# A four-layer graph network on one core: layer 2's edges in fixed chunks of 128, with the lock lookup moved into layer 1's experts

## The chip, the core and the metric

The kernel runs on one core of one Trainium2 chip. A core has a matrix unit (TensorE, PE; its loads of stationary operands are listed as PEld), VectorE (DVE), ScalarE (ACT), GpSimd (POOL) and SyncE (SP), each with an instruction list of its own that it works off in order, and DMA queues which are filled by SP, ACT and GpSimd. The metric is the device time of one execution, in microseconds (us). All data is fp32 unless said otherwise.

## The reference, cut to what matters

3125 nodes with 256 features, 100000 edges (source, destination, weight), sorted by destination. A layer is a graph convolution plus a mixer, added to x, and then a mixture of experts, added to x. Four such layers follow each other, of different kinds. The change touches two places: layer 1's experts, which every node passes through (8 experts, three 256 x 256 products each),

```
h = relu(bn(x @ W1[e] + b1[e])); h = relu(bn(h @ W2[e] + b2[e])); x += w[e] * (h @ Wo[e] + bo[e])
```

and the graph convolution of layer 2, which prunes small messages except into locked nodes:

```
norm_node_in = norm(x, axis=0);  norm_all_in = norm(norm_node_in) / 256
W_eff  = where(abs(W) < 0.1 * norm_all_in / norm_node_in, 0, W)
h      = x @ W_eff.T
lock   = locked[dst] | (src == dst)
msg    = edge_weight[:, None] * h[src]
n      = norm(msg, axis=1)
msg    = where((n < 0.1 * sum(n) / E) & ~lock, 0, msg)
out    = segment_sum(msg, dst) + b
```

Here `locked` marks the nodes of a list of 1000. The destinations are drawn as 3125 times the square of a uniform number, so low-numbered nodes have far more edges than high-numbered ones. Destinations and sources are known only on the device; what the program knows when it is built is their distribution.

## The kernel before

**Blocks and pieces.** Nodes lie in 25 blocks of 125 (`x[125, 25, 256]`, one node per partition), and are handled in seven pieces of four blocks (the last piece has one). `xt` is the same with the features on the partitions.

**PSUM.** `bank()` gives out PSUM banks from one pool of four in turn. A bank is free again when the instruction that reads its product out has run. The graph convolution of layer 2 has two accumulators of its own (`acc`).

**Layer 1's experts** (`l1_ffn`). For each expert and piece: products into h1, ScalarE evacuates them with the relu (L1411), products into h2, ScalarE again (L1416), then one product per block, which VectorE adds into x (L1422, scalar_tensor_tensor). The weights of an expert are loaded ahead from SP and ACT. After the last expert each piece is normed and transposed for layer 2 (`last`), one piece behind.

**Layer 2's preparation** (`l2_prepare`) is a generator which `l1_ffn` advances twice. First, before the experts, it issues the loads: GpSimd fetches the edge records (packed destination and source, and the weight) with 25 indirect DMAs, one per block (L1445), each with room for the most edges that the block can have. `ROOM` holds these sizes, in columns of 128 edges: 841 columns in all, where 100000 edges need 782; the rest is filled with edges of other blocks, which no target of the block matches. Second, after expert 1, it builds the lock table: `locked` from eight small products (L1464), then `lock`, one row of 125 flags per block broadcast over the partitions (L1471, L1473). The decoding of the records (L1477 to L1488) is written there too, but in VectorE's list it stands before the first update of the first expert.

**Layer 2's graph convolution** (`l2_gnn`). Fourteen Squares over `xt` on ScalarE (L1503) give the norms, W is pruned, h is computed per block and written to DRAM with its row norm as a 257th column (`hx`). Then the gather loop: for each block, in groups of up to eight columns (`CPG`), GpSimd gathers 128 rows of `hx` per column (L1551) into `hg`, of which there are four buffers. VectorE forms `keep` for the group (L1555, L1556) from the row norms, and for each column the 128 x 125 matrix `to`: first weight where the edge's target is this column of the block (L1560, tensor_scalar), then times the larger of lock and keep (L1562, scalar_tensor_tensor). PE multiplies `to` with the gathered rows into the block's accumulator (L1564; each fp32 product is two instructions in the profile). At the end of a block VectorE adds the accumulator into x (L1566).

**Order of the work.** `together` runs the gather loop and layer 2's mixer as two generators and always advances the one that reports the smaller share done. Each engine's list then follows from the order in which the program emits instructions, moved a little by the tool that lays them out; on the chip every engine takes its list in order and waits on semaphores. `prep`, at the very start, finds the first edge of each block and counts violations of the assumed room in `viol`; if there is one, the program at the end runs `general`, a second version of the network without such assumptions.

Of the kernel before, what the change touches and what calls it, by code (L numbers as in the profile page):

```python
# [12 lines left out]
F32 = mybir.dt.float32  # L13
I32 = mybir.dt.int32
# [3 lines left out]
AF = mybir.ActivationFunctionType  # L18
OP = mybir.AluOpType
AX = mybir.AxisListType  # L20
PSUM = bass.MemoryType.PSUM
DRAM = bass.MemoryType.DRAM

N = 3125
D = 256
P = 125
NB = 25
HB = D // 128
E = 100000
# [13 lines left out]
def _room(d0, d1):  # L43


    m = E * (math.sqrt(d1 / N) - math.sqrt(d0 / N))
    return max(1, math.ceil((m + 4 * math.sqrt(m) + 1) / 128))
# [18 lines left out]
NT1 = -(-NE1 // 128)  # L66
ROOM = [_room(b * P, b * P + P) for b in range(NB)]
NC2 = sum(ROOM)

# [19 lines left out]
class Net:  # L89
    NE, TS = 16, 384  # L90

    def __init__(self, tc, a, ctx):
# [13 lines left out]
        nc.vector.memset(self.ones, 1.0)  # L106
        self.iota_f = c.tile([128, 128], F32, name="iota_f")
        nc.gpsimd.iota(self.iota_f, pattern=[[1, 128]], base=0, channel_multiplier=0,
                       allow_small_or_imprecise_dtypes=True)
# [170 lines left out]
    def prep(self):  # L280

        nc, a = self.nc, self.a
        self.rec_d = self.dram.tile([1, 2 * EP], F32, name="rec_d")
        self.viol = self.c.tile([128, 8], F32, name="viol")
        self.tab = self.c.tile([128, 4, NT1 + 1], F32, name="tab")
        self.idx1 = self.c.tile([128, NT1], I32, name="idx1")
        self.idx2 = self.c.tile([128, NB], I32, name="idx2")
        nc.vector.memset(self.viol, 0.0)
        nc.scalar.dma_start(self.tab, nc.inline_tensor(_tables(), name="windows").ap())
        room = np.stack([np.broadcast_to(np.array(ROOM) * 128.0, (128, NB)),  # L290
                         np.arange(128)[:, None] * 2.0 * np.array(ROOM)], 1).astype(np.float32)
        with ExitStack() as s:
            sb = s.enter_context(self.pool("p_sb"))
            wk = s.enter_context(self.pool("p_wk", 3))
            rm = sb.tile([128, 2, NB], F32, name="rm")
            nc.scalar.dma_start(rm, nc.inline_tensor(room, name="room").ap())
            dst = sb.tile([128, EC], I32, name="dst")
# [70 lines left out]
            gap2 = sb.tile([128, NB], F32, name="gap2")  # L368
            nc.vector.tensor_sub(gap2, sr[:, 1:], sr[:, :NB])
            nc.vector.tensor_tensor(gap2, gap2, rm[:, 0, :], op=OP.is_gt)  # L370
            nc.vector.tensor_reduce(self.viol[:, 2:3], gap2, axis=AX.X, op=OP.add)
            i2 = sb.tile([128, NB], F32, name="i2")
            nc.vector.scalar_tensor_tensor(i2, sr[:, :NB], 2.0, rm[:, 1, :], op0=OP.mult, op1=OP.add)
            nc.vector.tensor_scalar(self.idx2, i2, float(2 * EP - 1024), None, op0=OP.min)

# [982 lines left out]
    def l1_ffn(self, before, after):  # L1358
# [4 lines left out]
        with ExitStack() as s:  # L1363
# [25 lines left out]
            def last(i, w):  # L1389
                self.norm_turn_piece(i, w)  # L1390

                x = self.x[:, i // P:(i + w) // P]
                nc.vector.tensor_add(x, x, self.e2["bias"][:P, None, :].to_broadcast([P, w // P, D]))

            self.expect(2, follow, 1)
# [36 lines left out]
    def l2_prepare(self, sb, wk):  # L1432
# [3 lines left out]
        e = self.e2 = {}  # L1436
        e["w"] = self.load_w(sb, "L2_gnn_W")
        li = wk.tile([P, LOCKS // P], I32, name="li", bufs=1)
        nc.scalar.dma_start(li, a["L2_gnn_node_lock"])
        bias = self.load_b(sb, "L2_gnn_b")  # L1440
        bo = self.load_b(wk, "L2_mix_b_out", eng=nc.sync)
        rec = wk.tile([128, NC2, 2], F32, name="rec_b", bufs=1)
        c0 = np.cumsum([0] + ROOM).tolist()
        for b in range(NB):
            nc.gpsimd.indirect_dma_start(  # L1445
                out=rec[:, c0[b]:c0[b + 1]].rearrange("p c t -> p (c t)"), out_offset=None, in_=self.rec_d,
                in_offset=bass.IndirectOffsetOnAxis(ap=self.idx2[:, b:b + 1], axis=1))
        yield
# [10 lines left out]
        for j in range(LOCKS // P):  # L1459
# [4 lines left out]
            nc.tensor.matmul(ps[:P, :NB], ol, oh, start=(j == 0), stop=(j == LOCKS // P - 1))  # L1464
        locked = sb.tile([P, NB], F32, name="locked")
        nc.vector.tensor_scalar(locked, ps[:P, :NB], 0.0, None, op0=OP.is_gt)

        lock = sb.tile([128, NB, P], F32, name="lock")
        for b in range(NB):
# [3 lines left out]
            nc.scalar.copy(lock[:, b, :], ps[:, :P])  # L1473
        pk = rec.bitcast(I32)[:, :, 0]
        idx = sb.tile([128, NC2], I32, name="idx")
        rel = sb.tile([128, NC2], F32, name="rel_b")
        nc.vector.tensor_scalar(idx, pk, 4095, None, op0=OP.bitwise_and)  # L1477
        nc.vector.tensor_scalar(idx, idx, N - 1, None, op0=OP.min)
        dI = wk.tile([128, NC2], I32, name="dI", bufs=1)
        nc.vector.tensor_scalar(dI, pk, 12, None, op0=OP.arith_shift_right)  # L1480
        same = sb.tile([128, NC2], F32, name="same")
        nc.vector.tensor_tensor(same, idx, dI, op=OP.is_equal)
        for b in range(NB):
            nc.vector.tensor_scalar(rel[:, c0[b]:c0[b + 1]], dI[:, c0[b]:c0[b + 1]], float(-P * b), None, op0=OP.add)
        wgt = sb.tile([128, NC2], F32, name="wgt")
        nc.vector.tensor_copy(wgt, rec[:, :, 1])
        awt = sb.tile([128, NC2], F32, name="awt")
        nc.vector.scalar_tensor_tensor(awt, wgt, -1.0, wgt, op0=OP.mult, op1=OP.max)  # L1488
        e.update(lock=lock, idx=idx, rel=rel, same=same, wgt=wgt, awt=awt, c0=c0)
        yield  # L1490

    def l2_gnn(self, sb, wk, pa):
        nc, tc, a = self.nc, self.tc, self.a
        hx = self.dram.tile([N, D + 1], F32, name="hx_d")
        w, lock, idx, rel, same, wgt, awt, c0 = (
            self.e2[k] for k in ("w", "lock", "idx", "rel", "same", "wgt", "awt", "c0"))

        ss = sb.tile([128, HB], F32, name="ss")
        sp = sb.tile([128, HB, len(PIECES)], F32, name="sp")
        for k, (i, n) in enumerate(PIECES):  # L1500
            for h in range(HB):
                sq = wk.tile([128, PW], F32, name="sq", bufs=1)
                nc.scalar.activation(sq[:, :n], self.xt[:, h, i:i + n], AF.Square, accum_out=sp[:, h, k:k + 1])  # L1503
        nc.vector.tensor_reduce(ss, sp, axis=AX.X, op=OP.add)
# [39 lines left out]
        yield 0.05  # L1544
        for b in range(NB):
            ps = pa.tile([P, D], F32, name="acc")
            for c in range(c0[b], c0[b + 1], CPG):
                m = min(CPG, c0[b + 1] - c)
                hg = wk.tile([128, CPG, D + 1], F32, name="hg", bufs=4)
                for j in range(m):  # L1550
                    nc.gpsimd.indirect_dma_start(  # L1551
                        out=hg[:, j, :], out_offset=None, in_=hx,
                        in_offset=bass.IndirectOffsetOnAxis(ap=idx[:, c + j:c + j + 1], axis=0))
                keep = wk.tile([128, CPG], F32, name="keep")
                nc.vector.tensor_mul(keep[:, :m], hg[:, :m, D], awt[:, c:c + m])  # L1555
                nc.vector.scalar_tensor_tensor(keep[:, :m], keep[:, :m], lim, same[:, c:c + m],  # L1556
                                               op0=OP.is_ge, op1=OP.max)
                for j in range(m):
                    to = wk.tile([128, P], F32, name="to", bufs=16)
                    nc.vector.tensor_scalar(to, self.iota_f[:, :P], rel[:, c + j:c + j + 1],  # L1560
                                            wgt[:, c + j:c + j + 1], op0=OP.is_equal, op1=OP.mult)
                    nc.vector.scalar_tensor_tensor(to, lock[:, b, :], keep[:, j:j + 1], to,  # L1562
                                                   op0=OP.max, op1=OP.mult)
                    nc.tensor.matmul(ps, to, hg[:, j, :D], start=(c + j == c0[b]), stop=(c + j == c0[b + 1] - 1))  # L1564
                yield 0.05 + 0.95 * (c + m) / NC2
            nc.vector.tensor_add(self.x[:, b, :], self.x[:, b, :], ps)  # L1566
            if b % 4 == 3 or b == NB - 1:
                self.arrive(b // 4 * PW)

    def l2_gnn_mix(self):  # L1570
        with ExitStack() as s:
            ms = s.enter_context(self.pool("m2_sb"))
            mw = s.enter_context(self.pool("m2_wk", 2))
            sb = s.enter_context(self.pool("g2_sb"))
            wk = s.enter_context(self.pool("g2_wk", 2))
            pa = s.enter_context(self.pool("g2_ps", 2, space=PSUM))
            mix = self.l2_mix_by_pieces(ms, mw)
            next(mix)
            self.expect(2, self.norm_turn_mean)
            self.together([self.l2_gnn(sb, wk, pa), mix])  # L1580
# [777 lines left out]
```

## Time and profile before

| | |
|---|---|
| time, median of 3 runs (lowest to highest) | 4976.61 us (4968.51 to 4979.73) |
| the profiled execution: its own time, its span | 4833.9 us, 4832.1 us |
| PE busy, share of the span | 3790.8 us, 78% |
| VectorE busy | 2451.3 us, 51% |
| ScalarE busy | 1322.7 us, 27% |
| GpSimd busy | 1122.3 us, 23% |
| mean granted PE clock | 0.857 |

The profile is of one execution. A row of its groups gives the source line, the engine, the operation with output and inputs, the shapes and the count; then the busy time of the group and the mean length of one; then how long the engine had been idle ahead of these instructions and what ended most of that idleness ("issue" means nothing that the profile shows). The stages that the change touches, in us from the start of the span: first expert from 1676, the lock table at 1822 to 1834, the following experts to 2238, the pruning and h to 2281, the gather loop from 2281 to 3365, the begin of layer 2's experts at 3424.

### The profile page before, as it was taken

The numbers are of one execution on the slowest core, as the hardware profiler recorded it, in microseconds if no ns is written. First come the engines' busy times: TensorE is split into PE (matmuls) and PEld (weight loads), VectorE is DVE, ScalarE is ACT, GpSimd is POOL, SyncE is SP. The second block draws the span as 40 slices with busy tenths as digits, with TensorE's granted clock in tenths as the row PEclk, the third lists the DMA queues.
The fourth block names the chain that finished last, engine by engine and source line by source line (L and its number), as shares of the span: only waits on it lengthen the run. The fifth ranks groups of instructions, "written<-read, shape, count | busy, mean of one in ns | idle before, by whom it ended". The sixth has DMA issues, their size and how long they took to land. (4 is left out here: it accounts for less than half of the span.)

```text
span 4832.1 us, 49604 instructions
## 1 busy us (share of the span) xinstructions
PE 3790.8 (78%) x16425; PEld 2514.1 (52%) x16425; DVE 2451.3 (51%) x7872; ACT 1322.7 (27%) x2364; POOL 1122.3 (23%) x1124
## 2 busy tenths in 40 slices
PE   1887796699747799998565565665699999999798
PEld 0676795467534556555444444444464444444465
DVE  5877325454476421115444444555265666667544
ACT  1466100111123223333000000000155655456521
POOL 1000002200143100000777777776000000000011
PEclk8686896799868799999777777777799999999699
DMA  6244611443231000001333333334201112112232
GB/s 176 66 118 125 144 49 32 128 123 112 86 81 27 25 7 14 13 7 45 100 104 104 103 103 104 103 102 121 81 7 36 50 48 54 45 45 53 56 122 65
DMA packets 256290, 360.32 MB, mean 75 GB/s; under 512 B 62959, under 2 KB 199096, under 8 KB 256027
## 3 DMA queue, kind: packets, MB, share of 16 engines
q1 hardware_dynamic: 132514, 168.96, 12.3%
q0 software_dynamic: 66480, 135.56, 10.6%
q10 hardware_dynamic: 57033, 52.54, 4.0%
q8 instruction: 135, 2.21, 0.2%
q14 instruction: 128, 1.05, 0.1%
HBM read 270.31 MB, written 94.92 MB: 76 GB/s over the span
## 5 line engine op out<-in xcount | busy, mean ns | idle before, releaser
L1564 PE MATMUL acc<-hg,to 128*125 128x256 f32 x1682 | 588.4, 517 | 422.3 <-DVE to L1562 401.7
L1551 POOL DMA_INDIRECT hg<-hx_d,idx x841 | 825.5, 982 | 298.2 <-issue 249.5
L1564 PEld LDWEIGHTS acc<-hg,to 128*125 128x125 f32 x1682 | 431.1, 265 | 566.3 <-DVE to L1562 473.0
L1905 PE MATMUL acc<-z,xr 125*65 125x500 f32 (+1 forms) x1400 | 576.3, 554 | 10.6 <-DVE z L1902 9.1
L1902 DVE SCALAR_TENSOR_TENSOR z<-t,us,cs 125x1000 f32<-125x1000 f32 (+1 forms) x400 | 410.1, 1029 | 139.5 <-PE acc L1905 102.9
L1899 ACT ACTIVATE t<-xn,us 125x1000 f32<-125x1000 f32 (+1 forms) x400 | 409.5, 1037 | 237.4 <-DVE z L1902 232.7
L1905 PEld LDWEIGHTS acc<-z,xr 125*65 125x65 f32 x1400 | 188.6, 144 | 314.1 <-issue 270.1
L1422 DVE SCALAR_TENSOR_TENSOR x<-ps,lg,x 125x256 f32<-125x256 f32 x200 | 93.8, 483 | 412.6 <-PE ps L233 412.6
L1555 DVE TENSOR_TENSOR keep<-hg,awt 128x8 f32<-128x8 f32 (+6 forms) x117 | 19.4, 166 | 553.2 <-DMA hg<-hx_d,idx 419.7
L239 PE MATMUL ps<-xt,w 128*128 128x500 f32 (+1 forms) x672 | 272.1, 552 | 8.7 <-DVE x L1422 7.0
L1560 DVE TENSOR_SCALAR to<-iota_f,rel_b,wgt 128x125 f32<-128x125 f32 x841 | 269.9, 361 | 1.2 <-PE acc L1564 0.6
L1562 DVE SCALAR_TENSOR_TENSOR to<-lock,keep,to 128x125 f32<-128x125 f32 x841 | 252.4, 344 | 0.0
L2188 POOL DMA_INDIRECT bx_d<-row,slot x25 | 31.4, 1255 | 930.1 <-ACT t L1899 812.3
L571 PE MATMUL ps<-y,cb 125*125 125x256 bf16 x1875 | 215.2, 280 | 0.0
L571 PEld LDWEIGHTS <-cb 125*125 125x125 bf16 x1875 | 213.9, 141 | 0.3 <-DMA cb<-cnt_d 0.2
L779 ACT ACTIVATE k<-k 125x128 f32<-125x128 f32 x50 | 15.9, 317 | 720.5 <-DVE k L778 668.9
L168 ACT ACTIVATE rstd_t<-rstd_t 125x4 f32<-125x4 f32 (+2 forms) x86 | 17.3, 204 | 674.5 <-DVE rstd_t L167 562.8
L233 PE MATMUL ps<-wo,h 128*125 128x256 f32 x800 | 187.7, 386 | 3.6 <-ACT h L1416 2.6
L239 PEld LDWEIGHTS ps<-xt,w 128*128 128x128 f32 x672 | 123.9, 195 | 123.6 <-issue 110.0
L239 PE MATMUL ps<-h,w 128*128 128x500 f32 (+1 forms) x448 | 178.2, 540 | 1.3 <-ACT h L1411 1.3
L233 PEld LDWEIGHTS ps<-wo,h 128*125 128x125 f32 x800 | 142.8, 187 | 66.0 <-ACT h L1416 43.7
L239 PE MATMUL pl<-xbt,w 128*128 128x384 f32 x416 | 168.9, 555 | 8.2 <-DVE xbt L1135 5.8
(558 smaller groups left out, 6295.4 us busy)
## 6 DMA issues: line engine op xcount, KB each, us to landing
cs<-ctt_d SPq DMA_DIRECT2D x150, 218.8 KB
w<-in_L_ffn_w_dram SPq DMA_DIRECT2D x52, 512.0 KB
cnt_d<-cd SPq DMA_DIRECT2D x25, 683.6 KB
cb<-cnt_d SPq DMA_DIRECT2D x25, 683.6 KB
ctt_d<-ct ACTq DMA_DIRECT2D x6, 2734.4 KB
hg<-hx_d,idx POOLq DMA_INDIRECT x841, 2.8
b0x_d<-zero SPq DMA_DIRECT2D x1, 9984.0 KB
xb<-b0x_d SPq DMA_DIRECT2D x26, 384.0 KB
```

The source lines that it names most:

```text
L233: self.nc.tensor.matmul(ps, xt[:, h, b * P:(b + 1) * P], w[:, h, :], start=(h == 0), stop=(h == k - 1))
L239: self.nc.tensor.matmul(ps, w[:, h, :], xt[:, h, i:i + n], start=(h == 0), stop=(h == k - 1))
L571: nc.tensor.matmul(ps[:P, :D], cf[k][:, h * P:(h + 1) * P], y3[:, b0 + k, j, :], start=(k == 0 and j == 0), stop=(k == m - 1 and j == 2))
L1422: nc.vector.scalar_tensor_tensor(self.x[:, b, :], ps[:P, :D], g[:, b, e:e + 1], self.x[:, b, :], op0=OP.mult, op1=OP.add)
L1551: nc.gpsimd.indirect_dma_start(out=hg[:, j, :], out_offset=None, in_=hx, in_offset=bass.IndirectOffsetOnAxis(ap=idx[:, c + j:c + j + 1], a ...
L1560: nc.vector.tensor_scalar(to, self.iota_f[:, :P], rel[:, c + j:c + j + 1], wgt[:, c + j:c + j + 1], op0=OP.is_equal, op1=OP.mult)
L1562: nc.vector.scalar_tensor_tensor(to, lock[:, b, :], keep[:, j:j + 1], to, op0=OP.max, op1=OP.mult)
L1564: nc.tensor.matmul(ps, to, hg[:, j, :D], start=(c + j == c0[b]), stop=(c + j == c0[b + 1] - 1))
L1899: nc.scalar.activation(t[:, :n], rows[:, k4, :n], AF.Relu, bias=us[:, 2, b, k4:k4 + 1], scale=us[:, 0, b, k4:k4 + 1])
L1902: nc.vector.scalar_tensor_tensor(z[:, :n], t[:, :n], us[:, 1, b, k4:k4 + 1], c, op0=OP.add, op1=OP.mult)
L1905: nc.tensor.matmul(acc[h, k][:, :w], xr[:, b, k4, :], z[:, k * PW:k * PW + w], start=(b == 0), stop=(b == NB - 1))
L2188: st = nc.gpsimd.indirect_dma_start(out=bx, out_offset=bass.IndirectOffsetOnAxis(ap=slot[:, j:j + 1], axis=0), in_=row[:, j, :], in_offset ...
```

## The change

1. **Chunks as they come.** The edges are no longer fetched by block. Column c holds edges 128c to 128c + 127, 782 columns in all. `SPANS` gives for each column the one or two blocks whose edges it can hold, from the distribution with 4.5 standard deviations: 543 columns have one block, 239 two. A column with two blocks gets a 128 x 250 matrix and two products, into both blocks' accumulators, of which there are now three; 1021 products in all. `prep` checks the block starts against the same tolerance. Two plain DMAs from SP load the records with 128 edges along the free dimension, and 21 transposes on PE bring them onto the partitions.
2. **The lock lookup.** Instead of multiplying lock flags into every mask, VectorE looks up the lock flag of every edge once in `l2_prepare`, after expert 1 of layer 1: one scalar_tensor_tensor with an accumulated sum per column, 782 of them, into `lk`. In the gather loop the kept weight `kw` of the group then takes three small operations, and the mask is one tensor_scalar per column. `lock` and `locked` need no room after that.
3. **The Squares** of layer 2's norms are taken piece by piece at the end of layer 1's last expert.

```diff
+def _starts():
+    q = np.sqrt(np.arange(NB) * P / N)
+    return E * q, 4.5 * np.sqrt(E * q * (1 - q)) + 2
...
-NC2 = sum(ROOM)
+NC2 = -(-E // 128)
+    for c in range(NC2):
+        bs = [b for b in range(NB) if at[b] - off[b] < 128 * c + 128
+              and (b == NB - 1 or at[b + 1] + off[b + 1] > 128 * c)]
+        out.append((bs[0], len(bs)))
@@ l1_ffn, last(i, w) @@
+                for h in range(HB):
+                    nc.scalar.activation(self.e2["sq"][:, :w], self.xt[:, h, i:i + w], AF.Square,
+                                         accum_out=self.e2["sp"][:, h, i // PW:i // PW + 1])
@@ l2_prepare, first part @@
-        for b in range(NB):
-            nc.gpsimd.indirect_dma_start(
-                out=rec[:, c0[b]:c0[b + 1]].rearrange("p c t -> p (c t)"), out_offset=None, in_=self.rec_d,
-                in_offset=bass.IndirectOffsetOnAxis(ap=self.idx2[:, b:b + 1], axis=1))
+        nc.gpsimd.memset(rec[:, nt - 1], 0.0)
+        nc.sync.dma_start(rec[:, :nt - 1].rearrange("p k e t -> p k (e t)"),
+                          flat[:128 * (nt - 1)].rearrange("(k p) t -> p k t", p=128))
+        nc.sync.dma_start(rec[:m, nt - 1].rearrange("p e t -> p (e t)"), flat[128 * (nt - 1):])
@@ l2_prepare, second part @@
+        for out, op, k in ((fr, OP.bitwise_and, 4095), (to, OP.arith_shift_right, 12), (wgt, None, None)):
+            if op is not None:
+                nc.vector.tensor_scalar(part, pk, k, None, op0=op)
+                nc.vector.tensor_copy(whole, part)
+            for t0 in range(0, nt, 4):
+                ps = self.bank()
+                for t in range(t0, min(nt, t0 + 4)):
+                    nc.tensor.transpose(ps[:, (t - t0) * 128:(t - t0 + 1) * 128],
+                                        rec[:, t, :, 1] if op is None else whole[:, t], self.ident)
+                nc.vector.tensor_copy(out[:, 128 * t0:128 * t0 + n], ps[:, :n])
...
+        for c, (b, m) in enumerate(SPANS):
+            junk = wk.tile([128, 2 * P], F32, name="junk")
+            nc.vector.scalar_tensor_tensor(junk[:, :m * P], self.iota_w[:, :m * P], rel[:, c:c + 1],
+                                           lock[:, b:b + m].rearrange("p b n -> p (b n)"), op0=OP.is_equal,
+                                           op1=OP.mult, accum_out=lk[:, c:c + 1])
+        nc.vector.tensor_tensor(to, fr, to, op=OP.is_equal)
+        nc.vector.tensor_tensor(lk, lk, to, op=OP.max)
@@ l2_gnn, the gather loop @@
-                nc.vector.scalar_tensor_tensor(keep[:, :m], keep[:, :m], lim, same[:, c:c + m],
-                                               op0=OP.is_ge, op1=OP.max)
+            nc.vector.scalar_tensor_tensor(kw[:, :m], kw[:, :m], lim, lk[:, c0:c0 + m], op0=OP.is_ge, op1=OP.max)
+            nc.vector.tensor_mul(kw[:, :m], kw[:, :m], wgt[:, c0:c0 + m])
...
-                    to = wk.tile([128, P], F32, name="to", bufs=16)
-                    nc.vector.tensor_scalar(to, self.iota_f[:, :P], rel[:, c + j:c + j + 1],
-                                            wgt[:, c + j:c + j + 1], op0=OP.is_equal, op1=OP.mult)
-                    nc.vector.scalar_tensor_tensor(to, lock[:, b, :], keep[:, j:j + 1], to,
-                                                   op0=OP.max, op1=OP.mult)
-                    nc.tensor.matmul(ps, to, hg[:, j, :D], start=(c + j == c0[b]), stop=(c + j == c0[b + 1] - 1))
+                to = wk.tile([128, nb * P], F32, name=f"to{nb}", bufs=10 if nb == 1 else 6)
+                nc.vector.tensor_scalar(to, self.iota_w[:, :nb * P], rel[:, c:c + 1], kw[:, j:j + 1],
+                                        op0=OP.is_equal, op1=OP.mult)
+                for k in range(b, b + nb):
+                    if c == first[k]:
+                        acc[k] = pa.tile([P, D], F32, name="acc")
+                    nc.tensor.matmul(acc[k], to[:, (k - b) * P:(k - b + 1) * P], hg[:, j, :D],
+                                     start=(c == first[k]), stop=(c == last[k]))
+                    if c == last[k]:
+                        nc.vector.tensor_add(self.x[:, k, :], self.x[:, k, :], acc.pop(k))
@@ l2_gnn_mix @@
-            pa = s.enter_context(self.pool("g2_ps", 2, space=PSUM))
+            pa = s.enter_context(self.pool("g2_ps", 3, space=PSUM))
```

## The prediction

> **What bounds the kernel now.** I read the page's groups first, then the time by stage, then the order of single instructions at the two places that the change touches. From the page (line, engine, operation, output and inputs, count, then busy time and mean length, then the engine's idle time ahead of them with its releaser):
>
> ```profile
> L1564 PE MATMUL acc<-hg,to 128*125 128x256 f32 x1682 | 588.4, 517 | 422.3 <-DVE to L1562 401.7
> L1551 POOL DMA_INDIRECT hg<-hx_d,idx x841 | 825.5, 982 | 298.2 <-issue 249.5
> L1422 DVE SCALAR_TENSOR_TENSOR x<-ps,lg,x 125x256 f32<-125x256 f32 x200 | 93.8, 483 | 412.6 <-PE ps L233 412.6
> L1562 DVE SCALAR_TENSOR_TENSOR to<-lock,keep,to 128x125 f32<-128x125 f32 x841 | 252.4, 344 | 0.0
> ```
>
> In the gather loop the matrix unit idles for 402 us behind the mask builder (L1562), but the builder waits for the gathers, and GpSimd waits for nobody: its gaps are "issue". In layer 1's experts it is the other way round: VectorE (L1422) idles for the matrix unit. By stage (start:end, length, then busy time with counts of PE, PEld, DVE, ACT, POOL, granted clock, DMA share, GB/s):
>
> ```profile
> 1660.00:1697.00 37.00, 22.28 (x59) 12.34 (x60) 13.93 (x64) 5.71 (x10) 21.37 (x23) 0.65 0.26 70
> 1834.00:2238.00 404.00, 400.04 (x1323) 233.33 (x1321) 100.23 (x246) 127.35 (x187) 0.00 (x0) 1.00 0.03 8
> 2281.00:3365.00 1084.00, 653.06 (x2035) 494.67 (x2034) 514.68 (x2064) 17.93 (x64) 825.15 (x841) 0.77 0.38 103
> ```
>
> Experts 2 to 7 (1834 to 2238) are PE-bound at 99%. The gather loop (2281 to 3365) is GpSimd-bound. Its order in time:
>
> ```profile
> 2296.97 0.95 POOL L1551 DMA_INDIRECT hg<-hx_d,idx  x1 [0.30 <-issue]
> 2298.22 0.95 POOL L1551 DMA_INDIRECT hg<-hx_d,idx  x1 [0.30 <-issue]
> ```
>
> One gather per 1.25 us at best; over the loop (first start 2280.6, last 3361.1, 840 steps) 1.286 us.
>
> The third view is the order in time at the first expert, where VectorE decodes the edge records (VectorE's lines, then PE's):
>
> ```profile
> 1689.69 0.60 DVE L1477 TENSOR_SCALAR idx<-rec_b 128x841 int32<-128x841 int32 x1 [12.98 <-DMA rec_b<-rec_d,idx]
> ...
> 1695.89 1.65 DVE L1422 SCALAR_TENSOR_TENSOR x<-ps,lg,x 125x256 f32<-125x256 f32 x4
> ...
> 1685.75 3.72 PE L233 MATMUL ps<-wo,h 128*125 128x256 f32 x16
> 1696.43 6.31 PE L239 MATMUL ps<-xt,w 128*128 128x500 f32 x8 [6.96 <-DVE x L1422]
> ```
>
> This is the pattern I expect to return, larger. VectorE runs its list in order; while it decoded, four finished products sat in all four PSUM banks, the updates (L1422) that empty them were queued behind, and PE stood still for 6.96 us. The eight matmuls after it took 6.31 us where eight warm ones take 3.52 (order in time at 1834.1).
>
> [...] L1902 (scalar_tensor_tensor) takes 348 ns for 125 and 1256 for 1000 elements, 1.04 ns each. [...] no row here has the accumulating form. [...] L1551 has a median of 946 ns but sums to 825.5 us, 30 us above 841 medians[...].
>
> **The change, part by part.**
>
> 1. *Lookups (new L1530), 782 on VectorE.* The built order of the changed kernel puts all 782, without a break, between the updates of expert 1 and the first update of expert 2: 543 of 125 elements and 239 of 250. Price: the plain form is 344 ns (L1562) for 125 and, at 1.04 ns more per element, 474 for 250. The accumulating form adds a read; the nearest rows are those of the edge counting in the prologue (order in time):
>
> ```profile
> 33.45 1.03 DVE L327 TENSOR_SCALAR_CACHE_REDUCE junk<-g,tab 128x782 f32<-128x782 int32 x1
> 34.40 0.08 DVE L327 DVE_READ_ACCUMULATOR junk<-g,tab 128x1 f32 x1
> 34.42 1.03 DVE L327 TENSOR_SCALAR_CACHE_REDUCE junk<-g,tab 128x782 f32<-128x782 int32 x1
> ```
>
> The read starts 0.95 us after a 1.03 us operation, so 0.08 before its end, and the next operation 0.02 to 0.04 after it. Start to start a lookup is therefore 0.344 - 0.08 + 0.03 = 0.294 us, or 0.424. Sum: 543 x 0.294 + 239 x 0.424 = 159.6 + 101.3 = 261 us. Each waits for the lookup two before it (two scratch buffers), which ends after 0.40 to 0.53 us, before its turn at 0.59 to 0.85; so that wait is taken as free. Bounds: without any cost of the read, at the 0.255 us start to start that L1560 and L1562 show, 0.255 and 0.385, 230 us; at half rate 0.424 and 0.684, 394 us. I take 261.
> Behind them are queued the updates of expert 2 (now L1442). Who waits is PE, through the four banks: it does one piece of expert 2 (10.5 us), then stands. Nothing covers the rest.
>
> 2. *Transposes and copies in front of the lookups.* Before, PE took up expert 2 at 1834.1 and needed its fifth bank 10.5 us later, at 1844.6. Now 21 transposes follow (0.26 us each by L221's 8 instructions per four in 1.02 us): 5.5 us. VectorE adds six copies out of PSUM, a second pass over the records, the relative positions (2.1 us, as 1692.3) and the absolute weights (1 us), so the lookups start at about 1844.5. They end at 1844.5 + 261; with a 0.95 us comparison and a 0.48 us update the bank is free at 2107. Against 1844.6: 262.4; plus 2.8 us of cold clock (6.31 - 3.52): **+265**.
>
> 3. *Records by two plain loads from SP instead of 25 gathers.* The 25 gathers of 1657 to 1687 held VectorE until 1689.7. The loads stand in SP's list behind one weight load and ahead of the four of the first experts; the bias loads there landed in 6 us, so I put the records' landing at 1665 to 1670, before the first expert. The decode moves behind expert 1 (part 2). PE's 7.0 us and the cold 2.8 go; a later first expert by about 1 us is possible: **-9**.
>
> 4. *Squares moved into the last expert.* 14 of 0.74 us on ScalarE at 2236.9 to 2246.8; the last input was ready at 2242.6, so the sum comes 3.6 us sooner. In the last expert ScalarE evacuates h just in time, and two squares per piece can delay it by up to 1.5 us, six times: 0 to 9. I take 4. **0**.
>
> 5. *Fewer gathers, masks at one pass.* 841 - 782 = 59 gathers at 1.286: **-76**. VectorE per chunk goes from 0.51 us (two passes) to 0.255 or about 0.32; it isn't the bound. PE products go from 841 to 1021: 588.4/841 = 0.70 us each; where half the chunks are double that is 1.05 us per chunk plus 0.08 of mixing, under 1.286, and warm products take 0.47 (eight instructions in 1.89 us at 2613.5). Three instead of two accumulators keep both blocks open. The last group's masks are six passes instead of twenty: 3 us less at the end. ScalarE's list there now has two small loads more ahead of the last evacuation (2.2 and 1.5 us at 3398.6): 3 us more. **0**.
>
> Sum: 265 - 9 + 0 - 76 + 0 = **+180 us**, on the profiled execution 4833.9 to 5014. The timed runs have a median of 4976.6, 143 us more than that execution; I carry the difference over unscaled: **5157 us**. A measurement tells 0.2% (10 us) from no change.
>
> **Rivals.**
> (a) *The gather loop keeps its length.* If double chunks make PE late, GpSimd waits for its four buffers, and the 76 us don't come: 5233. For it: PE's 1.13 us plus cold clock lies near 1.286. Against: only runs of twelve chunks are double, the buffers hold 32 chunks, and GpSimd waited for PE 2.7 us in all.
> (b) *Lookups at half rate.* 394 instead of 261: 5290. [...] against it L1902's plain rate.
> (c) *Not slower, by the lookup's price.* Without the stall the sum is 180 - 261 = -81, so it breaks even where a lookup costs 81/782 = 0.10 us. VectorE can issue that fast: the 24 short L1484 passes took 2.10 us. Against: those have 18 to 68 elements; 125 at 1.04 ns are already 0.13 us. Were the block wholly hidden: 4896.
> (d) *The change doesn't do what it says*: a block start outside its tolerance would run the general path as well, a second network. The starts in the reference's input lie within 0.41 of the tolerance, so no chance is given.
>
> **How the numbers follow.** Forecast 0.70, own range 5115 to 5205 (230 us of lookups[...]; or 290 us and 15 us lost in the last expert); (a) 0.10, (b) 0.12, (c) 0.03, anything unnamed 0.05. Leaving out (b), (c) and most of the unnamed, 5090 to 5265 holds 0.81. Faster 0.03 (c), same 0.01, slower 0.96.
>
> **What would show it.** Right: one stretch of some 250 us after expert 1 in which PE is empty and VectorE full with one line; lookups at 0.29 and 0.42 us; 782 gathers at 1.25 to 1.30 us with "issue" ahead of them; no PE gap at the first expert. Wrong: PE busy during the lookups, lookups over 0.4 us, gathers waiting for the accumulator's matmuls, or a loop much shorter than 1005 us.

## The result, and the profile after

The changed kernel takes 5095.73 us (median of four runs, 5090.62 to 5104.15), the kernel before, run beside it, 4974.68 (4968.51 to 4979.73): ratio 1.0246, 95% interval 1.0225 to 1.0266, 121 us slower. The forecast was 5157 with a range of 5090 to 5265: right in sign, 61 us too high, below the own range of the likeliest case (5115 to 5205) and only 6 us inside the lower end of the whole range.

The profiled execution of after took 5091.74 us (span 5089.9), as long as its timed runs. That of before had been 143 us shorter than its timed runs, so the two first profiles differ by 258 us where the clock tells 121. Why is the subject of half the experiments.

From the page's groups of after (line, engine, operation, output and inputs, shapes, count, then busy time and mean ns, then idle time ahead with its releaser):

```profile
L1594 POOL DMA_INDIRECT hg<-hx_d,idx x782 | 743.2, 950 | 410.6 <-issue 210.5
L1610 PE MATMUL acc<-hg,to 128*125 128x256 f32 x2042 | 597.5, 449 | 269.7 <-issue 144.0
...
L1605 DVE TENSOR_SCALAR to<-iota_w,rel_b,kw 128x125 f32<-128x125 f32 (+1 forms) x782 | 251.5, 379 | 434.1 <-remote 262.4
L260 PE MATMUL ps<-xt,w 128*128 128x500 f32 (+1 forms) x672 | 271.0, 550 | 238.7 <-DVE x L1442 237.0
...
L1530 DVE SCALAR_TENSOR_TENSOR junk<-iota_w,rel_b,lock 128x125 f32<-128x125 f32 (+1 forms) x782 | 242.3, 376 | 0.0
```

The last two rows are the forecast stall: 782 lookups without an idle moment, and PE's 237 us behind the updates queued after them (L1442). The first three were not forecast: the masks (L1605) wait 434 us, mostly for a releaser that the trace can't name ("remote"), where the masks of before had waited 1.2 us.

By stage in after (start:end, length, then busy time with counts of PE, PEld, DVE, ACT, POOL, granted clock, DMA share, GB/s): first expert, lookups, experts 2 to 7, gather loop.

```profile
1660.00:1697.00 37.00, 30.93 (x85) 17.22 (x86) 11.29 (x40) 7.40 (x12) 0.00 (x0) 0.75 0.17 55
1829.00:2073.00 244.00, 7.29 (x25) 4.19 (x23) 244.00 (x1567) 2.30 (x3) 0.00 (x0) 0.52 0.00 1
2073.00:2472.00 399.00, 392.30 (x1288) 228.38 (x1288) 102.37 (x254) 130.92 (x202) 0.22 (x2) 0.99 0.03 10
2507.00:3626.00 1119.00, 663.67 (x2363) 508.36 (x2361) 342.33 (x1229) 17.24 (x62) 743.25 (x782) 0.74 0.35 92
```

PE is busy for 30.9 instead of 22.3 of the 37 us at the first expert, for 7 of the 244 us of lookups, and the loop is 1116 us from first to last gather: longer than the 1080 of the first profile of before, with 59 gathers fewer.

The order in time shows the lookups' price, from one start to the next 0.27 us (125 elements) and 0.40 (250):

```profile
1829.63 0.34 DVE L1530 SCALAR_TENSOR_TENSOR junk<-iota_w,rel_b,lock 128x125 f32<-128x125 f32 x1
1829.90 0.08 DVE L1530 DVE_READ_ACCUMULATOR junk<-iota_w,rel_b,lock 128x1 f32 x1
1829.90 0.34 DVE L1530 SCALAR_TENSOR_TENSOR junk<-iota_w,rel_b,lock 128x125 f32<-128x125 f32 x1
...
2066.08 0.46 DVE L1530 SCALAR_TENSOR_TENSOR junk<-iota_w,rel_b,lock 128x250 f32<-128x250 f32 x1
2066.48 0.07 DVE L1530 DVE_READ_ACCUMULATOR junk<-iota_w,rel_b,lock 128x1 f32 x1
2066.48 0.46 DVE L1530 SCALAR_TENSOR_TENSOR junk<-iota_w,rel_b,lock 128x250 f32<-128x250 f32 x1
```

543 x 0.270 + 239 x 0.400 = 242 us. The next lookup starts together with the accumulator read of the one before. So the read adds at most 0.015 us to the 0.255 us of the plain form (L1560 and L1562 before), and the accumulating form runs at (0.400 - 0.270) / 125 = 1.04 ns an element, the 1.04 ns of the plain form (L1902 before).

And the gather loop, in which all three engines stand at times (order in time, PE's weight loads left out; L795 is of the mixer):

```profile
2693.79 0.35 DVE L1605 TENSOR_SCALAR to<-iota_w,rel_b,kw 128x125 f32<-128x125 f32 x1 [4.55 <-remote]
2693.84 0.94 POOL L1594 DMA_INDIRECT hg<-hx_d,idx  x1 [0.30 <-issue]
2694.19 1.22 PE L1610 MATMUL acc<-hg,to 128*125 128x256 f32 x2 [3.68 <-issue]
2695.08 0.94 POOL L1594 DMA_INDIRECT hg<-hx_d,idx  x1 [0.30 <-issue]
2698.00 0.35 DVE L1605 TENSOR_SCALAR to<-iota_w,rel_b,kw 128x125 f32<-128x125 f32 x1 [3.87 <-remote]
2698.40 1.22 PE L1610 MATMUL acc<-hg,to 128*125 128x256 f32 x2 [3.00 <-DVE to L1605]
2700.09 0.35 DVE L1605 TENSOR_SCALAR to<-iota_w,rel_b,kw 128x125 f32<-128x125 f32 x1 [1.74 <-PE acc L1610]
2700.35 0.28 DVE L795 TENSOR_TENSOR k<-ps,kmrow 125x128 f32<-125x128 f32 x1
2700.41 0.94 POOL L1594 DMA_INDIRECT hg<-hx_d,idx  x1 [4.38 <-PE acc L1610]
```

A single mask every 4 us, PE idle between, GpSimd standing from 2696.03 to 2700.41, while the rows for these masks had long landed: at 2678.57 VectorE already forms the weights of their group (L1598) from them. What each waits for is a buffer that PE has to give back: a mask waits for the product ten masks before, the gather at 2700.41 for the last product of the group of rows whose buffer it takes. In the trace that product had ended by 2678.5, 22 us before the gather could start; at two other gathers of the loop (2563.7 and 2814.3) the same reading gives 27 us. The trace also records updates of semaphores, the counters through which one engine signals to another that it has finished. For PE's semaphore around this place (my reading; of the 811 updates that the loop's instructions should make, 674 are recorded; times in us):

```
2678.34 2678.38 2681.88 2688.87 2693.76 2697.97
2700.07 2700.11 2700.15 2700.19 2700.24 2700.28 2700.32 2700.36 2700.41 2700.45
```

Signals of finished products trickle, one in about 4 us, and then ten come within 0.4 us, 4 us after GpSimd had stopped issuing. Ten products can't end that close together: the two instructions of one take at least 0.43 us in this trace. So the products were done, and the signals had been held. There are 30 such bursts (four or more signals at most 0.06 us apart) in the loop of after. In the first profile of before there is none: of 4345 signals of PE all but the last two came 0.014 us after their product's end, as against 22 us at this gather.

### The profile page after: what moved, and what is told of

Same layout as the page of the kernel before. It is cut to its first block, busy times and chain, and to the rows that moved or that the text cites. A ratio compares the mean times of both kernels' runs of the same rounds, so it can differ in the third digit from the quotient of the medians.

```text
span 5089.9 us, 50698 instructions
## 1 busy us (share of the span) xinstructions
PE 3798.8 (75%) x16806; PEld 2529.9 (50%) x16806; DVE 2524.6 (50%) x8603; ACT 1321.2 (26%) x2364; POOL 1015.4 (20%) x1041
## 5 line engine op out<-in xcount | busy, mean ns | idle before, releaser
L1594 POOL DMA_INDIRECT hg<-hx_d,idx x782 | 743.2, 950 | 410.6 <-issue 210.5
L1610 PEld LDWEIGHTS acc<-hg,to 128*125 128x125 f32 x2042 | 444.8, 224 | 402.8 <-issue 181.1
L1953 PE MATMUL acc<-z,xr 125*65 125x500 f32 (+1 forms) x1400 | 573.5, 552 | 10.5 <-DVE z L1950 8.8
L1605 DVE TENSOR_SCALAR to<-iota_w,rel_b,kw 128x125 f32<-128x125 f32 (+1 forms) x782 | 251.5, 379 | 434.1 <-remote 262.4
L1953 PEld LDWEIGHTS acc<-z,xr 125*65 125x65 f32 x1400 | 187.9, 143 | 313.0 <-issue 271.2
L1442 DVE SCALAR_TENSOR_TENSOR x<-ps,lg,x 125x256 f32<-125x256 f32 x200 | 93.9, 482 | 403.4 <-PE ps L254 403.4
L1530 DVE SCALAR_TENSOR_TENSOR junk<-iota_w,rel_b,lock 128x125 f32<-128x125 f32 (+1 forms) x782 | 242.3, 376 | 0.0
L1431 ACT ACTIVATE h<-ps,bnb,bng 128x500 f32<-128x500 f32 (+1 forms) x112 | 80.4, 722 | 497.7 <-PE ps L260 497.7
```

Of the source, the lines that this page charges most:

```text
L1431: nc.scalar.activation(h1[:, f, :w], ps[:, :w], AF.Relu, bias=bn[0][1][:, e, f:f + 1], scale=bn[0][0][:, e, f:f + 1])
L1442: nc.vector.scalar_tensor_tensor(self.x[:, b, :], ps[:P, :D], g[:, b, e:e + 1], self.x[:, b, :], op0=OP.mult, op1=OP.add)
L1530: nc.vector.scalar_tensor_tensor(junk[:, :m * P], self.iota_w[:, :m * P], rel[:, c:c + 1], lock[:, b:b + m].rearrange("p b n -> p (b n)"), ...
L1594: nc.gpsimd.indirect_dma_start(out=hg[:, j, :], out_offset=None, in_=hx, in_offset=bass.IndirectOffsetOnAxis(ap=idx[:, c0 + j:c0 + j + 1], ...
L1605: nc.vector.tensor_scalar(to, self.iota_w[:, :nb * P], rel[:, c:c + 1], kw[:, j:j + 1], op0=OP.is_equal, op1=OP.mult)
L1610: nc.tensor.matmul(acc[k], to[:, (k - b) * P:(k - b + 1) * P], hg[:, j, :D], start=(c == first[k]), stop=(c == last[k]))
```

## Experiments

Two questions: is the stall worth what the trace says, and who makes the signals late, the change or something that before suffers from too? The runs below come from four sessions. In the first two, before took 4977.5 and 4967.3 us, in the last two 4826.4 and 4829.9; the first and the last were on the same chip, so it isn't one chip's property. These are called late and on-time sessions here, after what their traces showed.

**1. before_again: the kernel before, unchanged.**

> The kernel before, unchanged, for a second profile. The profiled execution of before took 4834 us, its timed runs 4975; in the profile of after the end-of-product signals of PE reach VectorE and GpSimd up to some 20 us late inside the gather loop (never in the first profile of before), and the loop is 1116 us for 782 gathers. Theory A: those late signals belong to the changed loop (fewer mask buffers, two products per mask); then this profile is like the first one, gather loop about 1080 us, and the 141 us between profile and timed runs lie elsewhere. Theory B: they come with the executions that are timed, whatever the kernel; then this profile is near 4975, its gather loop about 1080 + 141 = 1220 us, with GpSimd waiting for PE's accumulator at group borders. Ratio 1.000 either way.

4974.14 us, ratio 0.9998 (0.9988 to 1.0007), profiled execution 4973.7. Its loop is 1212.5 us, with 24 bursts of late signals. The waits of GpSimd's gathers, of the second profile of before (us in all, times, longest):

```profile
POOL hg L1551 <- issue: 245.0, 798, 1.9
POOL hg L1551 <- remote: 69.3, 18, 7.0
POOL hg L1551 <- PE acc L1564: 58.7, 20, 9.6
```

and of its first profile:

```profile
POOL hg L1551 <- issue: 249.5, 819, 0.3
...
POOL hg L1551 <- PE acc L1564: 2.7, 9, 0.3
```

Theory B holds: the late signals are no part of the change, and the gather loop holds 132 of the 140 us between the two profiles of before. The profile that the prediction was worked from was of an execution without them.

Two more things stand in the traces. First, PE's signals are not the only ones: in before_again 237 of VectorE's come late too, up to 7 us. An example (order in time, GpSimd and PE's weight loads left out):

```profile
2443.13 1.13 DVE L1562 SCALAR_TENSOR_TENSOR to<-lock,keep,to 128x125 f32<-128x125 f32 x4 [1.64 <-remote]
2444.53 0.40 DVE L1562 SCALAR_TENSOR_TENSOR to<-lock,keep,to 128x125 f32<-128x125 f32 x1 [0.27 <-DVE to L1562]
...
2447.37 1.22 PE L1564 MATMUL acc<-hg,to 128*125 128x256 f32 x2 [0.88 <-remote]
2448.79 1.22 PE L1564 MATMUL acc<-hg,to 128*125 128x256 f32 x2 [0.19 <-remote]
2450.22 1.22 PE L1564 MATMUL acc<-hg,to 128*125 128x256 f32 x2 [0.21 <-remote]
```

The masks had ended by 2444.93; the products start behind signals of VectorE at 2447.33, 2448.74 and 2450.17. In after none of VectorE's recorded signals is late. Second, the record itself thins out. In the first profile of before all signals of the loop are recorded, and a gather's landing adds 16.0 updates; in before_again 767 of PE's 892 and 1188 of VectorE's 1993 are, with 2.5 updates per gather, and in after it is 2.8 per gather. Whether the rest was merged on its way or lost to the recorder is not shown. So single delays read from these traces are uncertain; that waiting instructions start at the recorded signals is not.

**2. no_lookups: the lookups left out.**

```
-        for c, (b, m) in enumerate(SPANS):
-            junk = ...
-            nc.vector.scalar_tensor_tensor(junk[...], self.iota_w[...], rel[...], lock[...], ..., accum_out=lk[...])
+        nc.vector.memset(lk, 0.0)
```

> After without the 782 lookups (the table they fill is set to zero, so edges into locked nodes are pruned like all others; that part of the computation is left out). If the stretch between the updates of expert 1 and expert 2 stands on the path with its whole length, 5096 - 243 = 4853 us (4840 to 4865), ratio 0.976 to before. If something else would have held PE there, less is gained: over 4900.

4872.70 us, ratio 0.979 (0.975 to 0.982); expected 4853, and at most 4865. The first gather comes at 2274.9 instead of 2507.2, 232 us sooner; its loop was 1133.5 instead of 1116.0, which gives 17 back. So the lookups cost 223 us of time, and everything else of the change together gains 105, in a late session.

**3. spread: the same lookups in 42 batches behind the pieces of experts 2 to 7.**

```
                             if e == NE - 1:
                                 self.arrive(i)
+                            if e > 1:
+                                next(later)
...
+        for step in range(6 * len(PIECES)):
+            yield
+            n = 20 if PIECES[step % len(PIECES)][1] == PW else 11
+            for c in range(done, min(NC2, done + n)):
```

> After with the same lookups in batches of about 20 behind each piece of experts 2 to 7, where VectorE was busy 100 of 404 us. If it is the solid block, and not the lookups' own time, that costs: as without the lookups, 4853 us and up to 20 us more where a batch holds up an update: 4853 to 4875. If VectorE has no room there (20 lookups are 6 us in a piece of 9.6 us with 2 us of updates): over 4900.

4875.01 us, ratio 0.980 (0.977 to 0.983): 2 us from the run without any lookups. The cost of the block is gone, and the kernel is faster than before and after. By stage in spread, experts 2 to 7:

```profile
1825.00:2229.00 404.00, 396.86 (x1310) 231.34 (x1309) 337.24 (x1817) 132.57 (x204) 0.22 (x2) 1.00 0.04 10
```

VectorE is busy for 337 instead of about 100 us of the stage and PE still for 397 of 404. It was the placing that cost, not the lookups as such.

**4. masks16: 16 and 8 mask buffers instead of 10 and 6.**

```
-                to = wk.tile([128, nb * P], F32, name=f"to{nb}", bufs=10 if nb == 1 else 6)
+                to = wk.tile([128, nb * P], F32, name=f"to{nb}", bufs=16 if nb == 1 else 8)
```

> After with 16 and 8 mask buffers instead of 10 and 6. If the loop of after is slow because VectorE runs out of mask buffers while PE's signals come late: the loop falls from 1116 towards 1005 us, the time to 4985 to 5050. If the gathers' own four buffers wait for the same late signals, as the waits of GpSimd for the accumulator say (88 us in 37 waits), the loop stays at 1100 or more and the time within 15 us of 5096.

5107.30 us, loop 1124.4: nothing gained. The masks' idle time falls from 434 to 250 us, and the same pauses stay with GpSimd.

**5. hg6: six instead of four buffers of gathered rows, on spread.**

```
-            hg = wk.tile([128, CPG, D + 1], F32, name="hg", bufs=4)
+            hg = wk.tile([128, CPG, D + 1], F32, name="hg", bufs=6)
```

> The spread version with six instead of four buffers of gathered rows. In all profiles but the first one of before, PE's end-of-product signals trickle while gathers are issued back to back and come in one burst a few us after GpSimd has stopped at a buffer border; with four buffers GpSimd stops after 24 gathers (30 us) for about 4.2 us. Theory: with six it stops after 40; the loop falls from 1138 to 782 x 1.25 + 20 x 4.2 = 1062 us, the time from 4875 to about 4800. Rival: VectorE, which waits for the same signals through its 10 mask buffers, keeps PE behind by as much as before: loop over 1110, time over 4850.

4863.43 us, loop 1122.4 where 1062 was expected. The theory fell, and these are the numbers that the text gives to its rival: behind the first stretch GpSimd still stops after mostly 24 or 16 gathers, 40 times in all. Deeper buffers alone don't space the pauses out; the masks, which wait for the same signals, idled 622 us here.

**6. grouped: one mask tile for eight chunks, so one wait for PE per group, on spread.**

```
+            wide = max(nb for _, nb in SPANS[c0:c0 + m])
+            tos = wk.tile([128, CPG, wide * P], F32, name=f"tos{wide}", bufs=2)
...
-                to = wk.tile([128, nb * P], F32, name=f"to{nb}", bufs=10 if nb == 1 else 6)
+                to = tos[:, j, :nb * P]
```

> The spread version with one mask tile for a group of eight chunks, two of each width, so that VectorE waits for PE once a group instead of at each mask. Theory that GpSimd's own four row buffers set the pauses: loop 1115 to 1145, time within 15 us of 4875. Rival, that VectorE's single waits for late signals hold PE back: loop under 1090, time under 4830.

4854.52 us, ratio 0.977 (0.974 to 0.980), loop 1117.9. The masks' idle time drops to 81 us and GpSimd's pauses stay (38, 138 us beyond the usual 0.30 of each). The loop is as the theory said, the time 5 us below its band. It is the fastest of the four of its session by a little. So the masks' waits alone don't make the pauses, and in hg6 the row buffers alone didn't either. No run lifted both limits at once; what that would give is open.

**7. single: one product per chunk, on spread.**

```
-        out.append((bs[0], len(bs)))
+        out.append((bs[0], 1))
```

> The spread version in which every chunk makes the mask and the product of its first block alone, 782 products instead of 1021 and no mask of 250; edges into the second block are left out of the sum. Rival (a) of the prediction, that double chunks make PE late: loop falls from 1138 to about 1005, time 4740 to 4760. If late signals and not PE's work hold GpSimd: loop 1100 to 1145, time 4840 to 4880.

4868.10 us, loop 1113.0 against 1137.6, in 782 products instead of 1021. Rival (a) of the prediction, PE late through double chunks, would have brought 1005. It didn't.

**8. paced: a memset on GpSimd after every gather, on spread.**

```
                         in_offset=bass.IndirectOffsetOnAxis(ap=idx[:, c0 + j:c0 + j + 1], axis=0))
+                nc.gpsimd.memset(pause, 0.0)
```

> The spread version with a memset of 128x256 (0.31 us on GpSimd) after every gather, so that a gather starts every 1.56 us instead of 1.25. If signals of PE pass only while GpSimd leaves a gap of some us, they stay late, and the pauses come on top: loop 782 x 1.56 + 130 = 1350, time about 5090. If it is the density of gathers (16 landing signals each 1.25 us) that delays them, they are on time at 1.56: no pauses, loop 1220, time about 4957.

4868.61 us, loop 1134.1, where 5090 or 4957 was expected, and the clearest trace of all, since it holds both cases. Some 120 of the memsets had no reason to wait and ran ahead of the loop, so that the first 112 gathers came bare. Order in time, early and later in the loop:

```profile
2342.03 0.95 POOL L1604 DMA_INDIRECT hg<-hx_d,idx  x1 [0.30 <-issue]
2343.28 0.95 POOL L1604 DMA_INDIRECT hg<-hx_d,idx  x1 [0.30 <-issue]
...
2600.09 0.95 POOL L1604 DMA_INDIRECT hg<-hx_d,idx  x1 [0.16 <-issue]
2601.03 0.34 POOL L1607 MEMSET pause<- 128x256 f32 x1
2601.53 0.95 POOL L1604 DMA_INDIRECT hg<-hx_d,idx  x1 [0.17 <-issue]
```

At 1.25 us per gather (to 2430) the next gather starts only 5 to 8 us after the one before at four places, behind 40, 64, 88 and 112 gathers, and all four bursts of this trace stand here. At 1.44 us per gather (from 2440 to 3405) there is no burst and no such pause; up to 2478 signals still come up to 6 us late, and from 2480 on none of 474 is more than 0.05 us behind its product. So in one and the same execution the signals are late while gathers come bare, and on time from some 45 us after the first memset between them. The landing updates change with it: 2.8 per gather in the bare stretch, 11.9 from 2480 on. That the first stretch is merely the begin of a loop is no explanation, since in after the bursts go on to the end. But whether it is the slower pace or something else about a memset between the gathers is not told apart by this run. The memset adds 0.19 and not 0.31 us, since half of the 0.30 between gathers goes; what the pauses had cost, the pace now costs.

**9. pace128 and pace192: shorter memsets, held behind the limit; before_pace128: the same in before.**

```
+        pause = sb.tile([128, 128], F32, name="pause")
+        nc.vector.tensor_copy(pause[:, :1], lim)
...
+                nc.gpsimd.memset(pause, 0.0)
```

> The spread version with a memset of 128x128 on GpSimd after every gather, held behind the pruning limit so that it can't run ahead of the loop. In the run with the 128x256 memset a gather came every 1.443 us (0.95 gather, 0.33 memset, 0.16 between), without a pause and with PE's signals on time; its first 112 gathers, ahead of which the memsets had already run, came every 1.251 us and had pauses and late signals. A 128x128 memset at about 0.20 us gives 0.95 + 0.20 + 0.16 = 1.31. Theory, that the density of gathers makes the signals late, with the limit below 1.31: loop 782 x 1.31 = 1024 us, no pauses, time 4875 - 113 = 4762. If the limit lies between 1.31 and 1.44: pauses return, loop 1110 to 1190, time 4850 to 4930.

> The same with 128x192, about 0.26 us, 1.37 per gather. If the limit lies below 1.37: loop 782 x 1.37 = 1071 us, time about 4810, without pauses. If not: over 4870.

> The kernel before with the 128x128 memset after every gather of its loop. If the difference between its first profile (4834) and its timed runs (about 4972) is the pauses of late signals: loop 841 x 1.31 = 1102 instead of 1212 us, time about 4862, ratio 0.978. If the difference is something else: the memsets only add, 4972 or more.

4827.83 us (1.000, 0.999 to 1.001), 4847.47 (1.005, 1.003 to 1.006) and 4913.30 (1.018, 1.016 to 1.020), all against a before of 4826.4. This was an on-time session: none of the three traces has a burst, every signal of PE in their loops comes 0.014 us after its product, and there is nothing that a memset could mend: before is 87 us slower with it (spread without memsets was not run here). Gathers come at 1.34 us in pace128 and 1.39 in pace192 (medians). So these runs say nothing on how slow a gather must be in a late session; between 1.25 and 1.44 that stays open.

**10. half_paced: after, with memsets of 128x48 from gather 392 on.**

```
+                if c0 >= NC2 // 2:
+                    nc.gpsimd.memset(hg[:, j, :48], 0.0)
```

> After, unchanged up to the middle of the gather loop; from gather 392 on each gather is preceded by a memset of 128x48 on GpSimd (0.15 us) into the buffer that it then fills. Two kinds of chips have been seen: on two of them before takes 4967 to 4977 us and PE's signals are late while gathers come every 1.25 us; on a third, before takes 4826 us and they never are. On a chip of the first kind: first half 392 x 1.43 = 560 us with pauses; second half, if a pace of about 1.35 is slow enough for the signals, 390 x 1.35 = 527 us without pauses, time about 5066; if not, pauses stay, 597 us, time about 5136. On a chip of the second kind: first half 392 x 1.286 = 504 us without pauses, second half 527; against before the block of lookups adds 230, the loop takes 1031 instead of 1080: before + 177, about 5003, ratio 1.037, which would be the +180 of the prediction's sum less 18 for cheaper lookups and plus 25 for the memsets.

4987.62 us against 4829.9, ratio 1.033 (1.031 to 1.035): an on-time session again, expected 5003. "Kinds of chips" in that text was wrong: the chip is the one of the first session, which had been late. The first half of the loop is the loop of after undisturbed, 494.4 us or 1.261 a gather; the second half is 520.4, or 1.338. The waits of the gathers here:

```profile
POOL hg L1596 <- issue: 201.7, 649, 2.0
...
POOL hg L1596 <- PE acc L1612: 3.6, 7, 1.8
```

With signals on time GpSimd does not wait for PE, double chunks or not. Less the memsets' (1.338 - 1.261) x 390 = 30 us, after would take about 4958 in an on-time session, 128 more than before: an estimate from this run, since after itself was not run in one.

## Why the prediction was right, and by how much it was off

The sum by its steps, against both pairs of traces: after and before_again (both late), half_paced and the first profile of before (both on time). Borders are the last update of expert 1, the first and last of experts 2 to 7, the first and the last gather.

| step | predicted | late pair | on-time pair |
|---|---|---|---|
| 1 and 2, lookups and what stands ahead of them | +265 | +242.7 | +242.2 |
| 3, records by plain loads | -9 | -10.1 | -10.9 |
| experts 2 to 7 | 0 | +2.0 | +1.9 |
| 4, squares | 0 | -5.1 | -5.0 |
| 5, gather loop | -76 | -96.5 | -65.6, or -95 less 30 us of memsets |
| behind the last gather | 0 | -15.1 | -10.4 |
| sum | +180 | +117.9 | +152.2, or +122 less the memsets |

1. *Lookups.* Right in mechanism, place and bounds (230 to 394). The lookups are 242 us instead of 261: I had the next one start 0.03 us after the accumulator read has begun, and it starts with it. The other 4 us of the term are what stands ahead: the lookups begin at 1829.6 instead of 1844.5, and 10 of these 15 us are step 3's gain; the 21 transposes take 2.9 us instead of the 5.5 that I had set.

2. *Cold clock.* Right: the first eight matmuls behind the stall take 6.05 us (predicted 6.31) at a mean granted clock of 0.59, the following ones run at 1.00; at the first expert of before it was 0.57 over the 6.31 us.

3. *Records.* Right: update 0 comes at 1685.1 (before_again 1695.3).

4. *Squares.* The term was mis-sized: 5 us gained from the last update to the first gather, where I had set 3.6 of gain against 4 of delay in the last expert. That delay is at most the 2 us of the row above it.

5. *Loop.* The number of gathers was right, their price was not: 59 x 1.443, as before's timed executions have it, is 85, and each of the other 782 became 0.014 us cheaper. In the on-time pair it is 59 x 1.286 = 76 and 782 x 0.025 = 19; in before 34 of 840 gathers had taken over 1.5 us from start to start, in the first half of half_paced one of 392. I had put L1551's time above its median at 30 us, and took none of it into the number. The traces have a sign of such losses: gathers that themselves take over 1.1 us are 46, 61 and 72 of 841 in the three traces of before's loop, with and without memsets, and at most 3 of 782 in every trace of the changed one. VectorE's second pass per column (L1562) is gone there, while its tensor_scalar passes only went from 841 to 782. No run tried either alone, so the cause is not shown.

6. *Behind the loop.* I had put it at nothing. It is 10 to 15 us less; 9 of them arise late, between the first product of L1905 (L1953 after) and the end, in code that the change doesn't touch, in both pairs. I did not follow that up.

*The carry-over.* The prediction added the 143 us between profile and timed runs of before unscaled, without knowing what they were. They are pauses of GpSimd behind late signals, and after pays nearly the same: its loop is 1116 against 986 us undisturbed (782 x 1.261), 130 us. So the step came out right, but by luck: the prediction had no reason for it, and had the changed loop been free of the pauses, the forecast would have been some 130 us further off. As it is, the difference of the change hardly depends on the kind of session: +121 measured in a late one, about +128 (the estimate above) in an on-time one.

*The ranges and the signs.* The own range doesn't follow from its terms: 31 us less for lookups of 230 us and the 30 that L1551 sums to above its medians, both in full, give 5096, not 5115, and 5096 is what was measured, though by another mix of terms. Of the signs for "right", the stretch without PE, the lookups (0.27 and 0.40 us) and the first expert without its gap came; gathers at 1.25 to 1.30 us did not, since with the pauses they average 1.43.

Of the rivals, (a) had the sign that I named for "wrong", gathers waiting for the accumulator's matmuls (88 us), but neither its cause (single, half_paced) nor its result: before waits in the same way. (b), whose half rate was an assumption of mine that no trace showed, and (c) fall with the price of 0.27 us.

The largest single error, about 23 of 61 us, is the lookups and their start; the loop's 20, the tail's 15 and the squares' 5 follow. All four point the same way, towards a higher time; the forecast was pessimistic throughout.

## What to carry to other kernels

Work that is small beside an engine's idle time can still cost all of its length when it stands as one block ahead of what another engine waits for: 242 us of lookups cost 223 in one place and 2 in pieces. Compare a profiled execution with the timed runs first; where they differ, profile the unchanged kernel again before the difference is carried into a forecast. When an engine is said to wait for one that had long been done, look at when the signal came, not only at when the work ended, and count whether all signals are in the record.

The version to take is spread, or grouped: 0.980 and 0.977 of before in late sessions. In an on-time session neither was run; from pace128 (4828 us, loop 1087) and a bare loop of 986 us, spread would take about 4727 there, an estimate.

## What the runs showed of the hardware that I had not expected

- PE's end-of-product signals can come over 20 us late (22 us at the gather shown, 27 at two others) while GpSimd issues gathers back to back, one per 1.25 us; at the gather shown they come in a burst, 0.04 us apart, 4 us after it stops. At 1.44 us per gather, with memsets between, they come on time in the same execution that had them late before (paced: from 2480 us on none of 474 more than 0.05 us behind its product). VectorE's can be late too, by up to 7 us (before_again). In the first profile of before, at 1.286 us per gather, all but two of 4345 came after 0.014 us; in half_paced, on the chip of the first session, 392 bare gathers took 1.261 us each, and the gathers waited 3.6 us for PE in the whole loop. The late signals cost about 130 us in both kernels (before's loop 1212.5 us in one profile and 1080 in the other, after's 1116 against an estimated 986).
- Where signals are late, the record of them is thin: 2.5 (before_again) to 2.8 (after) landing updates per gather instead of 16.0 (first profile of before) in the gather loops. What holds the signals is open; no run tried anything but memsets between the gathers, the buffers and PE's load.
- The accumulating scalar_tensor_tensor on fp32 takes 1.04 ns an element (after, L1530) as the plain form does (before, L1902): 0.270 us at 125 and 0.400 at 250 elements, start to start, 0.015 us more than the plain form's 0.255 at 125.
- A memset of 128x256 after a gather adds 0.19 us to its period (paced) and one of 128x128 about 0.09 (pace128), less than their own 0.33 and 0.22 us.
